# A selective scan's spread transfers on ScalarE's queue in the last image pair

## The chip, the cores and the metric

The program runs on one core of one Trainium2 chip. The metric is the device time of one execution in microseconds (us). Five engines each run their own instruction queue in order: PE (TensorE, matrix multiplies), DVE (VectorE), ACT (ScalarE), POOL (GpSimd) and SP (SyncE, which computes nothing and issues transfers). ACT can issue transfers too. Engines wait for each other, and for transfers, through semaphores.

## The reference

Eight images of 64 channels and 64 x 64 pixels pass through four layers: a bottleneck, two window-attention blocks, a dynamic filter with a convolution, and a vision state-space block. The change lies in the last one, in its selective scan. With `dt` the softplus of a projection of `x`, it computes for 4 directions, 128 channels and 16 states, along 4096 positions:

```
def step(h, inp):
    u_t, dt_t, B_t, C_t = inp
    h = h * jnp.exp(dt_t[..., None] * A) + dt_t[..., None] * B_t[:, :, None, :] * u_t[..., None]
    return (h, jnp.einsum('bkcn,bkn->bkc', h, C_t))
```

Every state of a channel needs that channel's `dt` and `dt*x`. After the scan the four directions are summed, normalized, gated and projected, and a last block (called `back` below) mixes the channels.

## The kernel before

Images are worked in four pairs. For pair p, `scans(p, ...)` (L1657) runs the scan of its two images while a generator named `beside` issues other work between the steps: the `back` of the pair before, and the `front` (all layers ahead of the scan) of the pair after. In the last pair there is no next pair, so `beside` holds only `back(2)`; when it is used up, `self.turn` becomes 0 (L1690) and tiles from `bank` alternate between the two sets of PSUM buffers. `late`, the last pair's own `back(3)`, is advanced only in the last seven units (L1693) and after the loop.

The scan of a pair is 64 units: 2 images x 4 directions x 8 chunks of 512 positions. A unit has 8 steps; a step handles 2 of the 16 states on 128 partitions (64 channels x 2 states, in two halves `j` of 512 columns). What one unit needs is made during the unit before it, after its first three steps (L1695):

- `load` (L1704), after step 0: a transfer of `x` into `xs`.
- `inputs` (L1709), after step 1: PE projects `x`; ACT makes the softplus (L1717, L1720) and copies `dt` into the tile `du1` (L1721); PE and ACT make the rows of B and C, which go to memory (`rows`, L1727).
- `spread` (L1729), after step 2: DVE multiplies `dt*x` into the second half of `du1` (L1733), then two transfers of 512 KB each (L1737) copy every channel of `du1` to two partitions of the tile `du`, one transfer for each half g of the channels. `du` has two buffers, `du1` one.

In each step, `fetch` (L1739) issues the broadcast transfers of the rows of B (three steps ahead) and of C (two steps ahead), with four buffers each; POOL multiplies B by `dt*x` from `du` (`products`, L1752, two steps ahead); ACT makes `exp(dt*A)` from `du` into a PSUM bank `dad` (L1774); DVE runs the recurrence (L1777); ACT copies the end of the recurrence to `carry` (L1785); DVE or POOL multiplies by C (L1791); PE sums over the states (L1803). After step 2 DVE gathers the unit before (L1816 to L1821).

All transfers of the scan are issued from SP's queue: B, C, `xs`, `rows`, `du` and the results. The order within each engine's queue isn't the written one alone: a planner lays the instructions out at build time by its own estimate of when each can start, and the earlier written one first where several can. [...]

Of the kernel before, what the change touches and what calls it, by code (L numbers as in the profile page):

```python
# [15 lines left out]
B, C, HH, WW = 8, 64, 64, 64  # L16
# [1143 lines left out]
class _Direct:  # L1160
# [568 lines left out]
    def spread(self, u):  # L1729

        nc, one = self.nc, u["one"]
        du = u["du"] = self.sw.tile([P, GRP, 2, TD], F32, name="du", tag="du")
        nc.vector.tensor_tensor(one[:, 1], u["pd"], u["x"], ALU.mult)  # L1733
        m = P // GRP
        for g in range(GRP):
            src = one[m * g : m * g + m].rearrange("c q t -> c (q t)").unsqueeze(1).to_broadcast([m, GRP, 2 * TD])
            nc.sync.dma_start(du[:, g].rearrange("p q t -> p (q t)"), src)  # L1737

    def fetch(self, i, st, s):  # L1739

# [213 lines left out]
```

## Time and profile before

| what | us |
|---|---|
| median of 3 executions | 12660.21 (12629.84 to 12661.61) |
| the profiled execution, of its own | 12668.15 |
| its span, first to last instruction | 12666.3 |

The last pair, by stretches of the profiled execution. Times are from the start of the span; shares are busy time over the stretch. Units are counted by their L1733, 64 in the pair.

| stretch, us | units prepared in it | beside the scan | DVE | POOL | ACT |
|---|---|---|---|---|---|
| 10422 to 10920 | 16 | first part of `back(2)` | 88% | 82% | 54% |
| 10920 to 11460 | 16 | its convolutions | 92% | 75% | 53% |
| 11460 to 11620 | 5 | its end | 89% | 82% | 50% |
| 11620 to 12310 | 21 | nothing | 80% | 79% | 44% |
| 12310 to 12530 | 6 | `back(3)` begins | 90% | 81% | 57% |

Over the whole span DVE is busy 67%, POOL 59%, ACT 55%, PE 77%. SP issues 512 `du` transfers, 128 of them in the last pair, with a median of 5.9 us from issue to landing. A line of the timeline names the start, the duration, the engine, the line of the program, what is written from what, and in brackets how long the engine had been idle and what ended that. SPq is SP's queue of transfers.

### The profile page before, as it was taken

What the parts mean: (1) busy time and instruction counts of PE and PEld (TensorE: products, weight loads), DVE (VectorE), ACT (ScalarE), POOL (GpSimd) and SP (SyncE); (2) the same over time, 40 slices, a digit from 0 to 9 for tenths busy, and PEclk for the clock granted to TensorE, in tenths of its full rate; (3) what the DMA queues carried; (4) which work ended last, traced back from release to release, by engine and by line L of the source; (5) the groups of instructions that cost most, each with busy time, mean ns of one, the idle gap of its engine ahead of it and who ended that gap; (6) DMA issues with size and microseconds to landing.
All of it is one profiled execution on the core that took longest, in us unless ns stands there. A gap on an engine that the chain in (4) does not pass through costs nothing. (4 is left out here: it accounts for less than half of the span.)

```text
span 12666.3 us, 142495 instructions
## 1 busy us (share of the span) xinstructions
PE 9810.4 (77%) x46358; PEld 3319.4 (26%) x46358; DVE 8518.4 (67%) x10259; ACT 7014.7 (55%) x15694; POOL 7504.2 (59%) x3844
## 2 busy tenths in 40 slices
PE   9888879987888667997988756998888855555456
PEld 2255222223342112222443211222433211111111
DVE  0122257678776776668776779467777678988878
ACT  5533237665654655666565555666666465455444
POOL 0000017677775683667676676467777568778774
PEclk9966779998888778998888867998888967777767
DMA  0000025554443463445443455344444356556554
GB/s 19 1 1 1 5 91 150 145 149 136 136 129 102 142 192 95 136 139 151 122 129 114 125 180 157 88 138 148 129 131 136 101 169 190 170 169 186 172 170 131
DMA packets 779701, 1575.82 MB, mean 124 GB/s; under 512 B 89280, under 2 KB 89408, under 8 KB 778176
## 3 DMA queue, kind: packets, MB, share of 16 engines
q1 hardware_dynamic: 754752, 1510.30, 40.1%
q10 hardware_dynamic: 24192, 56.32, 1.2%
q8 instruction: 367, 6.01, 0.2%
q14 instruction: 390, 3.19, 0.1%
HBM read 1197.16 MB, written 100.66 MB: 102 GB/s over the span
## 5 line engine op out<-in xcount | busy, mean ns | idle before, releaser
L1752 POOL TENSOR_TENSOR vd<-B,du 128x1024 f32<-128x1024 f32 x2048 | 4797.6, 2362 | 3280.0 <-DMA B<-rows 2024.8
L1803 PE MATMUL yd<-vd,pack 128*64 128x512 f32 x8192 | 2923.6, 736 | 939.0 <-POOL vd L1791 593.2
L1774 ACT ACTIVATE dad<-du,As 128x512 f32<-128x512 f32 x4096 | 2732.3, 682 | 1051.1 <-DVE hd L1777 409.0
L1777 DVE TENSOR_TENSOR_SCAN hd<-dad,carry,vd 128x512 f32<-128x512 f32 x1992 | 2498.3, 1268 | 485.6 <-ACT dad L1774 333.8
L1791 POOL TENSOR_TENSOR vd<-hd,C 128x512 f32<-128x512 f32 x1290 | 1646.5, 1281 | 1032.7 <-DVE hd L1777 1004.2
L1777 DVE TENSOR_TENSOR_SCAN dad<-dad,carry,vd 128x512 f32<-128x512 f32 x1592 | 2005.7, 1274 | 169.5 <-ACT dad L1774 165.4
L1788 POOL TENSOR_TENSOR vd<-hd,C 128x1024 f32<-128x1024 f32 x491 | 1158.3, 2359 | 712.9 <-DVE hd L1777 364.4
L1307 ACT ACTIVATE e<-s 128x512 f32<-128x512 f32 x2048 | 1201.6, 591 | 624.1 <-PE s L1301 622.3
L1301 PE MATMUL s<-X 64*128 64x512 f32 x4096 | 1429.7, 645 | 79.8 <-ACT e L1307 59.8
L1803 PEld LDWEIGHTS yd<-vd,pack 128*64 128x64 f32 x8192 | 658.3, 159 | 2796.3 <-issue 1197.4
L1791 DVE TENSOR_TENSOR vd<-dad,C 128x512 f32<-128x512 f32 x1824 | 1208.8, 674 | 268.0 <-ACT carry L1785 251.3
L1293 PE MATMUL po<-e,VT 128*64 128x512 f32 x4096 | 1209.8, 625 | 16.9 <-ACT e L1307 10.2
L1458 PEld LDWEIGHTS w_av<-vals,wide 64*64 64x64 f32 x16384 | 674.9, 172 | 201.8 <-ACT wide L1448 75.1
L1458 PE MATMUL w_av<-vals,wide 64*64 64x9 f32 x16384 | 703.3, 223 | 20.5 <-ACT wide L1448 20.3
L1785 ACT ACTIVATE carry<-hd 128x1 f32<-128x1 f32 (+1 forms) x1559 | 307.7, 200 | 690.8 <-DVE hd L1777 677.3
L1301 PEld LDWEIGHTS s<-X 64*128 64x128 f32 x4096 | 391.4, 186 | 1107.1 <-issue 834.5
L1785 ACT ACTIVATE carry<-dad 128x1 f32<-128x1 f32 x1594 | 268.3, 169 | 681.0 <-DVE dad L1777 671.0
L1715 PE MATMUL pdd<-xs,xdt 128*128 128x512 f32 x512 | 375.5, 823 | 326.1 <-issue 103.0
L1239 PE MATMUL pv<-n_sq,pack 128*128 128x512 f32 x576 | 361.8, 713 | 154.6 <-ACT n_sq L1237 142.8
L1448 ACT ACTIVATE wide<-wide 128x512 f32<-128x512 f32 x512 | 309.7, 626 | 279.3 <-DVE wide L1447 278.9
L1575 PE MATMUL acc<-taps,pack 128*128 128x512 f32 x576 | 374.1, 782 | 107.6 <-DVE taps L1574 107.2
L1447 DVE TENSOR_TENSOR wide<-w_s,bias 128x512 f32<-128x512 f32 x512 | 328.4, 680 | 191.2 <-PE w_s L1430 187.1
(246 smaller groups left out, 10620.4 us busy)
## 6 DMA issues: line engine op xcount, KB each, us to landing
B<-rows SPq DMA_DIRECT2D x2048, 256.0 KB, 3.5
C<-rows SPq DMA_DIRECT2D x2048, 256.0 KB, 3.5
du<-du SPq DMA_DIRECT2D x512, 512.0 KB, 5.9
xs<-xt SPq DMA_DIRECT2D x128, 256.0 KB, 3.7
xs<-xc SPq DMA_DIRECT2D x128, 256.0 KB, 3.8
xc<-xcv ACTq DMA_DIRECT2D x64, 256.0 KB, 2.0
zs<-z ACTq DMA_DIRECT2D x64, 256.0 KB, 3.8
xt<-XT ACTq DMA_DIRECT2D x32, 512.0 KB, 4.8
```

What stands on the lines that cost most here:

```text
L1293: nc.tensor.matmul(po[half[im]], lhsT=VT[:, t, half[im]], rhs=es[im], start=(t == 0), stop=(t == 31))
L1301: nc.tensor.matmul(ss[im], lhsT=at(half[im], t), rhs=X[half[im], jc * CH : (jc + 1) * CH], start=True, stop=True)
L1307: nc.scalar.activation(e, ss[im], AF.Exp, scale=C**-0.5, accum_out=parts[:, im, t, jc : jc + 1])
L1458: nc.tensor.matmul(self.av[half[im], x % 4 + j, h, :], lhsT=es[h // 4][half[im], j, h % 4, :], rhs=V[half[im], x + j, h, :], start=True, s ...
L1715: nc.tensor.matmul(pd, lhsT=net.xdt[:, k, :], rhs=x, start=True, stop=True)
L1752: self.nc.gpsimd.tensor_tensor(v, self.twice(st["B"]), self.units[i // 8]["du"][:, :, 1], ALU.mult)
L1774: nc.scalar.activation(da, u["du"][:, j, 0], AF.Exp, scale=net.As[:, k, n : n + 1])
L1777: nc.vector.tensor_tensor_scan(along(to), along(da), along(v[:, j]), first, ALU.mult, ALU.add)
L1785: nc.scalar.activation(cs, ends, AF.Copy)
L1788: st["w"] = nc.gpsimd.tensor_tensor(v, h, self.twice(CC), ALU.mult)
L1791: m = engine.tensor_tensor(v[:, j], hs[j], CC, ALU.mult)
L1803: m = nc.tensor.matmul(u["y"][self.HALF[j]], lhsT=w["fold"], rhs=st["v"][:, j], start=(i % 8 == 0), stop=(i % 8 == 7))
```

## The change

The two transfers of `spread` are issued from ACT's queue for images 6 and 7, which make up the last pair; for the others they stay on SP's.

```diff
         nc.vector.tensor_tensor(one[:, 1], u["pd"], u["x"], ALU.mult)
         m = P // GRP
+        queue = nc.scalar if u["image"] >= B - 2 else nc.sync
         for g in range(GRP):
             src = one[m * g : m * g + m].rearrange("c q t -> c (q t)").unsqueeze(1).to_broadcast([m, GRP, 2 * TD])
-            nc.sync.dma_start(du[:, g].rearrange("p q t -> p (q t)"), src)
+            queue.dma_start(du[:, g].rearrange("p q t -> p (q t)"), src)
```

Sizes, sources, destinations and the number of transfers are the same.

## The prediction

> **What bounds the kernel now.** Only the last pair's 64 units change, so I read that stretch alone: first who waits for whom, then the timeline of one unit. The waits between 11300 and 12300 us (engine and line, what it waited for; total us, times, longest):
>
> ```profile
> ACT dad L1774 <- DMA du<-du: 197.8, 45, 10.4
> POOL vd L1752 <- DMA du<-du: 145.0, 22, 7.7
> DVE vd L1791 <- ACT carry L1785: 125.6, 26, 7.0
> ```
>
> The spread transfer is what ACT and POOL wait for longest, and DVE waits for ACT about as long. The same view from 10300 to 11300 us gives POOL 25.3 us on `du` and ACT none worth listing: the wait belongs to the stretch with nothing beside the scan. One unit of it in the timeline:
>
> ```profile
> 11831.21 0.67 DVE L1733 TENSOR_TENSOR du<-pdd,xs 128x512 f32<-128x512 f32 x1
> 11831.81 2.45 DVE L1777 TENSOR_TENSOR_SCAN dad<-dad,carry,vd 128x512 f32<-128x512 f32 x2
> 11831.91 0.69 ACT L1774 ACTIVATE dad<-du,As 128x512 f32<-128x512 f32 x1 [0.96 <-DVE du L1733]
> ...
> 11834.39 0.56 SPq L1744 DMA_DIRECT2D B<-rows  x1
> ...
> 11839.62 0.51 SPq L1744 DMA_DIRECT2D C<-rows  x1
> ...
> 11840.18 0.60 SPq L1744 DMA_DIRECT2D B<-rows  x1
> ...
> 11840.88 1.20 SPq L1737 DMA_DIRECT2D du<-du  x2
> ...
> 11842.14 2.19 SPq L1744 DMA_DIRECT2D C<-rows  x1
> ...
> 11846.43 1.30 ACT L1774 ACTIVATE dad<-du,As 128x512 f32<-128x512 f32 x2 [7.22 <-DMA du<-du]
> ...
> 11847.85 0.69 DVE L1791 TENSOR_TENSOR vd<-dad,C 128x512 f32<-128x512 f32 x1 [5.93 <-ACT carry L1785]
> ...
> 11848.71 2.35 POOL L1752 TENSOR_TENSOR vd<-B,du 128x1024 f32<-128x1024 f32 x1 [6.67 <-DMA du<-du]
> ```
>
> What to see: the source of the spread is complete at 11831.88, but SP issues the transfers at 11840.88, 9.0 us later. SP isn't busy: it stands at a fetch of C whose buffer POOL frees only at 11839.6 (its L1791), and B and `du` are queued behind that. ACT then waits 7.22 us at the next unit's first exponential; the carry copies of the old unit stand behind it in ACT's queue, so DVE, which has old work ready, idles 5.93 us, and POOL 6.67 us.
>
> The timeline also holds the other case:
>
> ```profile
> 11577.07 0.69 DVE L1733 TENSOR_TENSOR du<-pdd,xs 128x512 f32<-128x512 f32 x1
> 11577.81 1.20 SPq L1737 DMA_DIRECT2D du<-du  x2
> 11587.09 2.36 POOL L1752 TENSOR_TENSOR vd<-B,du 128x1024 f32<-128x1024 f32 x1 [0.43 <-DMA B<-rows]
> ```
>
> Here SP was free, the transfers went out 0.05 us after the multiply, landed at about 11585, and neither ACT nor DVE stood still; POOL lost 0.43 us, on B. Going through L1733 and L1737 of the last pair this way: in the 22 units prepared from 11604 to 12325 us the issue comes 7.7 to 11.4 us late, and these units take 32.75 us each (720.5 us from the first L1733 to that of the 23rd). Just before, late and punctual units alternate: the intervals after punctual issues (0.1 to 2.7 us late) are 27.0, 26.7 and 26.3 us, those after late ones (8.1 and 8.8 us) 31.0 and 33.9 us.
>
> **What the Trainium skill says.** "DMA: Bandwidth & Descriptors", section on the anatomy of one DMA: a transfer's wait is done by the issuing sequencer before dispatch, not by the DMA engines. The trace agrees: the 9.0 us above pass ahead of the issue. The same page, "Issuing engines are not separate DMA queues": transfers from SP, ACT and POOL run on the same 16 DMA engines and interleave; another issuer saves only sequencer time. So I count no bandwidth won, only the queueing. Its section on queues and rings says that SP and ACT own one ring each on every DMA engine, served in turn by packets; the trace fits so far as fetches issued behind `du` take 2.2 us to issue (11842.14) where 0.5 is usual, which should go. "Perfetto Trace Analysis", on hardware-generated DMAs, says that the reported interval of an issue is the sequencer's own time; so 2 x 0.6 us is what ACT's queue would be held by each spread.
>
> **The change part by part.**
>
> *Removed from SP:* 128 issues of 0.6 us, on an engine that mostly waits. By itself nothing; B and C move up, and no fetch is issued behind a megabyte.
>
> *Moved to ACT:* two issues a unit, waiting for L1733. Price on ACT: 1.2 us a unit as on SP. (ACT's own 256 KB stores show 0.33 us as median, the 512 KB ones 0.62, so 0.65 to 1.25 us bounds it; I take 1.2.) In the quiet stretch ACT is 44% busy and lies idle 0.96 us until L1733 ends anyway. The next DVE work needing ACT: the two recurrences from 11831.81 have their exponentials already, and the one at 11835.36 needs the exponential of 11831.91, which would run at 33.1 to 33.8. So 0 there, if the planner puts the issues right at L1733.
>
> *Late wait gone:* punctual spreads in this pair (15 of the 64) landed 6.8 to 9.0 us after the multiply, the first half after 4.5 to 7.1. From 11831.9 that means 11836.4 to 39.0 and 11838.7 to 40.9. ACT wants the first half at 11839.2, POOL the whole at 11842.0. Both are met or missed by under 1 us; contention from the fetches can't be seen separately, and the punctual cases had it too.
>
> *What is late next:* without its 5.93 us of idle, that unit's 32.61 us (11815.24 to 11847.85) leave DVE 26.7 us of unbroken work; POOL's stretch from 11816.16 to 11842.04 is 25.9. Those are the floors. The two engines feed each other, and a small B wait appeared in the punctual unit, so I take 27.5 us, between 26.7 and the 28.6 us that the recurrences of that punctual unit spanned (11565.0 to 11593.6, 2.1 us of it idle). 22 units x (32.75 - 27.5) = 115.5 us. The two late units before them: 31.0 + 33.9 - 2 x 27.5 = 9.9 us. Together -125.
>
> *The other 40 units:* no gain that I count. In the 16 from 10422 the issue is 0 to 9 us late and POOL waits 5.5 us at B behind it, but DVE, 88% busy, waits for ACT, which waits 55.5 us in total at L1717 for PE; an earlier B doesn't end that. There I take +0.5 us a unit, within -2 and +2: ACT's exponentials come close on L1733 and 1.2 us more can show. In the 15 of the convolutions DVE is 92% busy; at 11034.6 the row copy and the exponentials stand right behind L1733 and DVE already waits 1.31 us for them, while at 11279.7 they are done. I take +0.8, within 0 and +2. In the last stretch, +0.5 for five units; the few in between I count at nothing. Sum 8 + 12 + 2.5 = +22.
>
> Net -125 + 22 = -103 on the profiled execution's 12668.15 us: 12565. The median shown lies 8 us under that execution, so 12557, say 12558.
>
> **The rivals.**
>
> *A second wait takes half.* POOL at 25.9 of 27.5 us a unit has little room; SP still stands at fetches of C until POOL frees a buffer, B sits behind them, and POOL may wait for B where it waited for `du`. For: the 0.43 us above, and the 65.5 us of B waits in POOL from 10422 to 10900. Against: there they came behind the `du` issues. With units at 30 us the gain is 22 x 2.75 = 60, less 22: 12668 - 38 - 8 = 12622.
>
> *The move doesn't do what it says.* The planner may set the issues late in ACT's queue, behind exponentials or copies that wait for DVE, or a semaphore shared with an earlier transfer holds them. Then `du` is as late as before: about 12650. Against: nothing on ACT between L1733 and its end needs anything but L1733.
>
> *Slower.* ACT's queue is in order, so from when it reaches the issues until L1733 ends it does nothing else. If the planner sets them ahead of the exponentials of step 3, DVE finds no `dad` after L1733 and idles for 1.2 us of issue plus 0.68 of exponential, about 2 us; beside `back`, whose squares, logarithms and Gelus also stand behind, more. It decides once it costs 125/63 = 2.0 us a unit; at 3 us, 189 - 125 = +64: 12724. For: ACT reaches that place early in the first two stretches. Against: in the quiet stretch and at 12398 the exponentials precede L1733.
>
> **How the numbers follow.** Chances: forecast 0.68, own range 12505 to 12605; second wait 0.15; no effect 0.08; slower 0.09. About 0.3%, or 38 us, is what a measurement can tell from no change, so faster means under 12622. The forecast and over half of the second wait are faster, 0.77; the rest of that and no effect are the same, 0.14; slower 0.09. Range: the floors (22 x 6.05 + 10 = 143), no cost elsewhere and a few us won among the first 16 units give 12500; upward it takes in the second wait and no effect up to 12655, leaving out the slower case and some tail below.
>
> **What would show it.** Right: the `du` issues on ACT within 0.2 us of L1733's end; no wait of 5 us or more for `du` on ACT or POOL between 11600 and 12300; unit spacing there 27 to 28 us; DVE over 93% busy there; the first two stretches as long as before within 2%. Wrong: exponentials that DVE waits for right after the issues, B in the place of `du` in POOL's waits, or ACT idle at the issues ahead of L1733.

## The result, and the profile after

| | median, us | all runs | profiled execution | its span |
|---|---|---|---|---|
| before | 12656.5 | 12629.84 to 12661.61 | 12668.15 | 12666.3 |
| after | 12524.3 | 12509.1 to 12532.55 | 12516.79 | 12515.0 |

The ratio is 0.9898, with a 95% interval of 0.988 to 0.9916: 1% faster. The granted TensorE clock is 0.82 in both profiles. The new line in the source moves everything below it by one: L1737 is now L1738, L1752 is L1753, L1774 is L1775, L1777 is L1778, L1785 is L1786 and L1791 is L1792.

First the waits of after between 11300 and 12300 us, the view that the prediction began with (total us, times, longest):

```profile
ACT carry L1786 <- DMA C<-rows: 50.9, 9, 8.0
...
POOL vd L1753 <- DMA du<-du: 30.8, 19, 2.7
...
DVE vd L1792 <- DMA C<-rows: 23.0, 20, 2.5
...
DVE vd L1792 <- ACT carry L1786: 12.0, 13, 2.8
```

ACT's 197.8 us at `du` are gone from the list, POOL's 145.0 have become 30.8 and none is longer than 2.7, and DVE's 125.6 us behind ACT's carry copies have become 12.0. One line is new: ACT standing ahead of carry copies until a fetch of C lands, 50.9 us. A carry copy doesn't read C; the timeline of one unit shows what this is.

```profile
11757.62 1.29 ACT L1775 ACTIVATE dad<-du,As 128x512 f32<-128x512 f32 x2
...
11759.16 0.67 DVE L1733 TENSOR_TENSOR du<-pdd,xs 128x512 f32<-128x512 f32 x1
11759.57 1.74 SPq L1745 DMA_DIRECT2D C<-rows  x2
...
11759.76 2.45 DVE L1778 TENSOR_TENSOR_SCAN dad<-dad,carry,vd 128x512 f32<-128x512 f32 x2
11760.19 3.41 ACTq L1738 DMA_DIRECT2D du<-du  x2
...
11762.12 1.25 DVE L1778 TENSOR_TENSOR_SCAN hd<-dad,carry,vd 128x512 f32<-128x512 f32 x1
11763.30 2.43 DVE L1778 TENSOR_TENSOR_SCAN dad<-dad,carry,vd 128x512 f32<-128x512 f32 x2
11763.64 0.23 ACT L1786 ACTIVATE carry<-dad 128x1 f32<-128x1 f32 x2 [4.73 <-DVE hd L1778]
...
11765.65 1.86 DVE L1792 TENSOR_TENSOR vd<-dad,C 128x512 f32<-128x512 f32 x3
...
11769.11 2.35 POOL L1753 TENSOR_TENSOR vd<-B,du 128x1024 f32<-128x1024 f32 x1 [1.27 <-DMA B<-rows]
```

The multiply ends at 11759.83 and the first transfer goes out 0.36 us later; over the quiet units the mean is 0.10 us, and the prediction had wanted 0.2. ACTq is ACT's queue of transfers. The ACTq line spans 3.41 us for two issues of 0.53: in the trace's events the second goes out at 11763.06, when the semaphore that it is to raise has been released by an earlier transfer, the fetch of C that SP had issued at 11759.57 (landed 11763.04). ACT does nothing for 4.73 us. DVE's recurrences nevertheless follow each other at 11759.76, 11762.12 and 11763.30 without a gap, since all the exponentials that they need were made ahead, the last two at 11757.62.

The quiet stretch as a whole, the 22 units from the 37th to the 59th L1733: length, then busy us (instructions) of PE, PE's weight loads, DVE, ACT and POOL, then clock, DMA share and GB/s. Before:

```profile
11604.00:12325.00 721.00, 367.87 (x796) 82.26 (x792) 580.30 (x618) 320.14 (x766) 567.20 (x308) 0.70 0.56 170
```

After:

```profile
11569.00:12168.00 599.00, 348.49 (x796) 76.15 (x796) 577.61 (x617) 311.92 (x765) 568.19 (x308) 0.69 0.67 205
```

The same work in 122 us less: DVE goes from 80% to 96% busy and POOL from 79% to 95%. From L1733 to L1733 the trace gives this for the pair:

| stretch (units of the last pair) | before, us | after, us | difference |
|---|---|---|---|
| up to the pair's first L1733 | 10422.3 | 10402.9 | -19.4 |
| 16 units beside the first part of `back(2)` | 498.5 | 500.8 | +2.3 |
| 15 beside its convolutions | 538.4 | 520.4 | -18.0 |
| 5 at its end | 144.9 | 144.7 | -0.2 |
| 22 quiet ones | 720.5 | 599.3 | -121.2 |
| 5 beside `back(3)` | 171.6 | 175.1 | +3.5 |
| the rest | 170.1 | 171.8 | +1.7 |

The first row is not put down to the change: up to there SP, ACT, DVE and POOL run the same instructions in the same order in both profiles (13395 on ACT, 8097 on DVE), and the profiles of nine other kernels below that leave that part alone reach this point anywhere from 10360 to 10410 us. The profile of before is the latest of all. The last pair itself gave 132 us.

One more thing differs in the last pair that the diff doesn't show: the planner laid the other engines' work out anew. In after, DVE runs five recurrences right after the multiply in 19 of the 22 quiet units (11759.76 to 11763.30 above). In before it runs two in all 22 and then multiplies by C, as in the punctual unit that the prediction showed:

```profile
11577.66 2.46 DVE L1777 TENSOR_TENSOR_SCAN dad<-dad,carry,vd 128x512 f32<-128x512 f32 x2
...
11580.02 1.28 DVE L1791 TENSOR_TENSOR vd<-dad,C 128x512 f32<-128x512 f32 x2
```

So a part of the gain may be owed to the new order and not to the spread. e4 and e7 below keep two recurrences after the multiply, and help to bound that part.

### The profile page after: what moved, and what is told of

The parts are those of the page before. It is cut to its first block, busy times and chain, and to the rows that moved or that the text cites. A ratio compares the mean times of both kernels' runs of the same rounds, so it can differ in the third digit from the quotient of the medians.

```text
span 12515.0 us, 142739 instructions
## 1 busy us (share of the span) xinstructions
PE 9804.9 (78%) x46358; PEld 3303.1 (26%) x46358; DVE 8519.5 (68%) x10259; ACT 7003.1 (56%) x15694; POOL 7502.7 (60%) x3844
## 5 line engine op out<-in xcount | busy, mean ns | idle before, releaser
L1753 POOL TENSOR_TENSOR vd<-B,du 128x1024 f32<-128x1024 f32 x2048 | 4797.0, 2362 | 3137.6 <-DMA B<-rows 2018.3
L1775 ACT ACTIVATE dad<-du,As 128x512 f32<-128x512 f32 x4096 | 2726.5, 682 | 863.2 <-DVE hd L1778 406.5
L1778 DVE TENSOR_TENSOR_SCAN hd<-dad,carry,vd 128x512 f32<-128x512 f32 x1992 | 2497.8, 1268 | 481.1 <-ACT dad L1775 324.4
L1792 POOL TENSOR_TENSOR vd<-hd,C 128x512 f32<-128x512 f32 x1290 | 1648.8, 1282 | 1032.3 <-DVE hd L1778 1018.2
L1778 DVE TENSOR_TENSOR_SCAN dad<-dad,carry,vd 128x512 f32<-128x512 f32 x1592 | 2003.9, 1274 | 160.8 <-ACT dad L1775 157.5
L1792 DVE TENSOR_TENSOR vd<-dad,C 128x512 f32<-128x512 f32 x1824 | 1207.2, 675 | 147.3 <-ACT carry L1786 112.6
L1293 PE MATMUL po<-e,VT 128*64 128x512 f32 x4096 | 1212.6, 626 | 16.9 <-ACT e L1307 10.2
L1786 ACT ACTIVATE carry<-dad 128x1 f32<-128x1 f32 x1594 | 266.5, 169 | 794.3 <-DVE dad L1778 698.7
L1786 ACT ACTIVATE carry<-hd 128x1 f32<-128x1 f32 (+1 forms) x1559 | 308.1, 200 | 672.7 <-DVE hd L1778 659.2
L1293 PEld LDWEIGHTS po<-e,VT 128*64 128x64 f32 x4096 | 234.8, 136 | 852.8 <-issue 569.8
```

The costliest lines, as they stand in the source:

```text
L1293: nc.tensor.matmul(po[half[im]], lhsT=VT[:, t, half[im]], rhs=es[im], start=(t == 0), stop=(t == 31))
L1753: self.nc.gpsimd.tensor_tensor(v, self.twice(st["B"]), self.units[i // 8]["du"][:, :, 1], ALU.mult)
L1775: nc.scalar.activation(da, u["du"][:, j, 0], AF.Exp, scale=net.As[:, k, n : n + 1])
L1778: nc.vector.tensor_tensor_scan(along(to), along(da), along(v[:, j]), first, ALU.mult, ALU.add)
L1786: nc.scalar.activation(cs, ends, AF.Copy)
L1792: m = engine.tensor_tensor(v[:, j], hs[j], CC, ALU.mult)
```

## The experiments

The main theory: `du` is late because its issue stands in SP's queue behind a fetch of C that waits for a buffer; a queue that is not standing there takes the wait away, and the quiet stretch is then bound by DVE and POOL. All spacings below are of the quiet stretch unless another is named, all differences in the pair are between its first and last L1733 (before 2073.8 us, after 1940.3).

### e1, e2 and e3: other sets of units

The condition of the change, `u["image"] >= B - 2`, becomes `u["image"] == B - 1` in e1 and `u["image"] == B - 2` in e2; in e3 it falls away:

```diff
-            nc.sync.dma_start(du[:, g].rearrange("p q t -> p (q t)"), src)
+            (nc.scalar if u["image"] == B - 1 else nc.sync).dma_start(du[:, g].rearrange("p q t -> p (q t)"), src)
```

> The spread transfers go on ACT's queue for image 7 alone (the last 32 units), image 6 stays on SP. Queue theory (the gain is the punctual spread in the quiet stretch, which lies in image 7): the quiet units fall from 32.75 to about 27.2 us, about -115 us in all, 12530 to 12555. Planner theory (the new order of the whole last pair gives the gain, wherever the transfers are issued): a part of the gain that follows the number of moved units, about -65 us.

> The spread transfers go on ACT's queue for image 6 alone, image 7 stays on SP. Queue theory: the quiet units stay at 32.7 us with the 6 us of idle DVE at each boundary; the time is within -25 and +15 us of before. Planner theory: about half of the gain, -65 us.

> The spread transfers go on ACT's queue in all four pairs. Queue theory: outside the last pair the trace of before has 22 us of waits for du in all, so there is nothing to win there, and ACT, busier with front work, pays 0 to 1.2 us for each of 192 units: between the time of the changed kernel and 200 us above it, 12520 to 12720. If a late spread were a cost in all pairs alike, it would fall well below 12500.

| kernel | median, us | ratio | 95% interval | last pair, us | quiet unit, us |
|---|---|---|---|---|---|
| e1, image 7 alone | 12533.58 | 0.9917 | 0.9901 to 0.9934 | 1953.6 | 27.21 |
| e2, image 6 alone | 12646.0 | 1.0004 | 0.9995 to 1.0013 | 2074.2 | 32.57 |
| e3, all four pairs | 12632.57 | 0.9987 | 0.998 to 0.9995 | 1942.8 | 27.24 |

Image 7 holds the quiet stretch, and moving its issues alone gives 120 of the 134 us, not a half, so the queue theory's forecast holds and the planner theory's, by the number of moved units, doesn't. (e1 has after's order on DVE in the quiet units, so it can't part the spread from that order.) Moving image 6's alone shortens the convolution stretch by 19 us, 538.4 to 519.2, and gives it all back in the next five units, 144.9 to 164.0: those are issued from SP again, and come 7.4 us late where they came 4.0 late before.

e3 answers whether the other queue is good in itself. The last pair is as short as after, but the first three are longer, by L1733: 2701.7, 2904.8 and 2912.4 us against after's 2680.1, 2872.4 and 2860.3. That is 106 us over 192 units; the whole time lies in the range that was expected. Their issues were only 1.0 us late on SP, so there was little to win; POOL's waits for `du` outside the last pair come to 54 us in before, where the expectation had counted 22. What it cost is in the waits over these three pairs (1832 to 10349 us in after, 1830 to 10461 in e3). After:

```profile
DVE hd L1778 <- ACT dad L1775: 335.0, 195, 10.7
DVE dad L1778 <- ACT dad L1775: 173.1, 157, 7.8
...
POOL vd L1753 <- DMA du<-du: 49.9, 19, 10.4
```

e3:

```profile
DVE hd L1777 <- ACT dad L1774: 401.0, 226, 9.1
DVE dad L1777 <- ACT dad L1774: 257.8, 160, 8.8
...
POOL vd L1752 <- DMA du<-du: 385.5, 44, 12.3
```

DVE waits 151 us more for ACT's exponentials; ACT, which also does the attention and layer work of the next pair there, now stands at issues too. `du` isn't even earlier: the whole of it lands 8.6 us after the multiply (median) where it was 7.2, because the second issue is 2.6 us late on average against 1.8, and POOL waits 336 us more for it. DVE doesn't pass that on: its recurrences in `hd` waited 143.4 us for POOL's products in after and 65.0 in e3. So the trace puts the loss at ACT. The planner's order changed in these pairs too, though, and no run parts the two. The net cost, 0.55 us a unit, is of the size of the 0.5 to 0.8 us that the prediction set as ACT's price.

### e4: SP again, but the spread ahead of the fetches

All transfers stay on SP, and in the last pair each later fetch is ordered behind the spread.

```diff
+            m_ = nc.sync.dma_start(du[:, g].rearrange("p q t -> p (q t)"), src)
+            self.spread_last = m_ if u["image"] >= B - 2 else None
...
-        self.nc.sync.dma_start(t, row.unsqueeze(0).to_broadcast([64, 2, TD]))
+        d = self.nc.sync.dma_start(t, row.unsqueeze(0).to_broadcast([64, 2, TD]))
+        if self.spread_last is not None:
+            self.net.behind(d, self.spread_last)
```

> All spread transfers stay on SP's queue, but in the last pair the later fetches of B and C are ordered behind them in that queue. Queue theory (only the place behind the standing fetches made them late): du is issued within 0.2 us of L1733's end, quiet units 27 to 28.5 us, 12520 to 12570, as good as the changed kernel within 0.4%. Rival (a queue of its own is needed, since now the fetches stand behind a wait for DVE and POOL runs out of B): POOL waits for B by several us a unit, quiet units over 30 us, 12600 or more.

Measured: 12555.45 us, ratio 0.9932 (0.9915 to 0.9948), 28.54 us a quiet unit: what the queue theory expected, at the upper end of its spacing. A unit of its timeline:

```profile
11660.12 0.69 DVE L1733 TENSOR_TENSOR du<-pdd,xs 128x512 f32<-128x512 f32 x1
...
11660.72 2.46 DVE L1780 TENSOR_TENSOR_SCAN dad<-dad,carry,vd 128x512 f32<-128x512 f32 x2
...
11660.87 1.20 SPq L1737 DMA_DIRECT2D du<-du  x2
11662.12 2.13 SPq L1745 DMA_DIRECT2D B<-rows  x1
...
11663.08 1.28 DVE L1794 TENSOR_TENSOR vd<-dad,C 128x512 f32<-128x512 f32 x2
...
11664.35 2.10 SPq L1745 DMA_DIRECT2D C<-rows  x1
```

The spread is 0.06 us late in the quiet units, ACT issues none of it, and both halves have landed 7.0 us after the multiply (9.0 in after). DVE runs two recurrences after the multiply in all 22 quiet units, as in before. So about two thirds of the gain, 0.0068 of 0.0102, came from the place in the queue, without another queue and without DVE's new order. Where the remaining 1.3 us a quiet unit lie isn't shown. The trace points at what is now behind the spread: B and C take 2.1 us to issue there instead of 0.5, and POOL waits for B (from 11500 to 12200 us):

```profile
POOL vd L1755 <- DMA B<-rows: 34.8, 16, 4.2
```

DVE in turn waits 37.6 us for POOL's products in e4's quiet stretch, and not at all in after's. In the quiet stretch 41 fetches take over 1.5 us to issue in e4, 43 in before and 14 in after. The other candidate is DVE's new order, which after has and e4 hasn't.

Ahead of the quiet stretch the two queues seem to differ: the 16 first units take 480.3 us in e4 and 500.8 in after, the 15 beside the convolutions 545.3 against 520.4. The two stretches are better read together. Over the 31 units before takes 1036.9 us, e4 1025.6, e6 (below) 1021.7 and after 1021.2. All three gain; how the gain divides between the two stretches differs from kernel to kernel.

### e6: one half on each queue

```diff
+            (nc.scalar if u["image"] >= B - 2 and g == 0 else nc.sync).dma_start(du[:, g].rearrange("p q t -> p (q t)"), src)
```

> In the last pair the first of the two transfers goes on ACT's queue, the second stays on SP's. Queue theory: POOL's products need both halves, so POOL waits as in before for the second, and ACT's exponentials for the second half of the channels too: quiet units 31 to 33 us, at most 35 us won. Rival (half the megabyte off SP's queue is enough, since the fetches behind it issue faster): about half of the gain, -60 us.

Measured: 12612.22 us, ratio 0.9978 (0.997 to 0.9986), 31.47 us a quiet unit, as the queue theory expected. The first half goes out 0.1 us after the multiply, the second, on SP, 7.8 us; POOL needs both halves at once, and its wait between 11500 and 12200 us stays what it was (118.8 us in before):

```profile
POOL vd L1752 <- DMA du<-du: 120.7, 21, 6.1
```

For POOL the spread is as early as its later half.

### e7: the slower rival, made

The changed kernel with the exponentials of step 3 ordered behind the issues, the order that the prediction's slower rival feared.

```diff
...
-            nc.scalar.activation(da, u["du"][:, j, 0], AF.Exp, scale=net.As[:, k, n : n + 1])
+            ex = nc.scalar.activation(da, u["du"][:, j, 0], AF.Exp, scale=net.As[:, k, n : n + 1])
+            if i % 8 == 3 and self.spread_last is not None:
+                net.behind(ex, self.spread_last)
```

> The changed kernel, with the exponentials of step 3 ordered behind the two issues in ACT's queue: the slower rival of the prediction, made on purpose. If an in-order hold of ACT at the issues costs what was worked out there, DVE idles after L1733 for at least 1.2 us of issue and 0.7 us of exponential in nearly all 64 units: 2 us a unit, +128 us over the changed kernel, about 12650; if ACT also stands between the two issues (2 to 3 us there in the trace of the changed kernel), 4 to 5 us a unit, 12750 to 12830. If ACT's place doesn't matter: within 30 us of the changed kernel.

Measured: 12541.05 us, ratio 0.9923 (0.9907 to 0.994), 28.49 us a quiet unit. One unit:

```profile
11722.29 0.69 DVE L1733 TENSOR_TENSOR du<-pdd,xs 128x512 f32<-128x512 f32 x1
...
11723.14 1.19 ACTq L1737 DMA_DIRECT2D du<-du  x2
...
11724.38 1.91 ACT L1775 ACTIVATE dad<-du,As 128x512 f32<-128x512 f32 x3 [3.27 <-POOL vd L1753]
11725.17 2.35 DVE L1780 TENSOR_TENSOR_SCAN dad<-dad,vd 128x512 f32<-128x512 f32 x2 [2.19 <-ACT dad L1775]
```

DVE idles 2.19 us after the multiply, 2.25 on the mean of the quiet units where it is 0.00 in after: the rival's 1.2 + 0.68 was well sized. But the unit grows by only 1.25 us, because the 0.97 us that DVE idles elsewhere in after are gone. The first 36 units together grow by 6.7 us and the pair by 29.0, to 1969.3 us, where the expectation had 128 or more if the hold costs. In this order the change still pays.

e7 also answers the question of DVE's order: its 616 DVE instructions of the quiet stretch stand in exactly the order of before, and with ACT's loss included it still wins 4.3 of the 5.5 us a unit.

### e8 and e12: carry copies first, on the kernel before

Is it rather ACT's order, with the old unit's carry copies behind the new unit's exponentials, that makes the late `du` expensive? Both kernels leave the spread on SP. e8:

```diff
...
+            ex = nc.scalar.activation(da, u["du"][:, j, 0], AF.Exp, scale=net.As[:, k, n : n + 1])
+            if i % 8 == 0 and self.carried is not None:
+                net.behind(ex, self.carried)
...
+                self.carried = nc.scalar.activation(cs, ends, AF.Copy)
+                if u["image"] < B - 2 or i % 8 < 7:
+                    self.carried = None
```

> The kernel before, with the first two exponentials of a unit ordered behind the last carry copy of the unit before, in the last pair; no transfer is moved. It takes away what made DVE stand still while old work was ready. If DVE's 6 us at the boundary are the cost: quiet units near 28 us, about -100 us. If the late spread itself is (POOL's products wait for it just as long, and POOL's 25.9 us of work plus 6.7 us of wait is the unit too): quiet units stay over 31 us, at most 35 us won.

Measured: 12635.73 us, ratio 1.0002 (0.9993 to 1.0011), 32.34 us a quiet unit. It first looked as if ACT's order didn't matter. But the edit hadn't made the order it was to make: the new unit's own first carry copy clears `carried`, so that the exponential of its second half wasn't held. The waits of DVE in e8's quiet stretch (11550 to 12260 us) show it:

```profile
DVE vd L1795 <- ACT carry L1787: 84.2, 19, 6.2
```

In before (11604 to 12325 us) these waits, and POOL's, were:

```profile
DVE vd L1791 <- ACT carry L1785: 121.0, 20, 7.0
...
POOL vd L1752 <- DMA du<-du: 140.7, 20, 7.7
```

Most of DVE's wait was still there, so e8 doesn't decide. e12 repairs it:

```diff
...
+            ex = nc.scalar.activation(da, u["du"][:, j, 0], AF.Exp, scale=net.As[:, k, n : n + 1])
+            if i % 8 < 3 and self.carried is not None:
+                net.behind(ex, self.carried)
...
+                copied = nc.scalar.activation(cs, ends, AF.Copy)
+                if u["image"] >= B - 2 and i % 8 == 7:
+                    self.carried = copied
```

> In e8 only the first of the new unit's exponentials was ordered behind the old unit's last carry copy, and the second still ran ahead of it, so DVE went on waiting for carry copies (84 us in the quiet stretch). Here all exponentials of the new unit's first three steps are ordered behind that copy, on the kernel before. If the lateness of du on its own is the bound, through POOL's products, DVE's wait for carry copies goes under 20 us but the quiet units stay at 31.5 us or more and the total within 25 us of before. If the order on ACT is what makes the lateness expensive, DVE's idle time of some 5.5 us a unit shrinks by half or more, units come to 30 us or less, and the total falls by 60 us or more.

Measured: 12606.4 us, ratio 0.9973 (0.996 to 0.9985), 30.74 us a quiet unit. DVE's and POOL's waits from 11560 to 12260 us:

```profile
DVE vd L1795 <- ACT carry L1787: 6.8, 12, 1.4
```

```profile
POOL vd L1752 <- DMA du<-du: 84.0, 18, 7.4
```

It falls between the two theories. With the issue still 7.3 us late (9.7 before) and on SP, e12 wins 2.0 of the 5.5 us a unit that the change wins: DVE's wait for carry copies is all but gone, and POOL's wait for `du` falls from 140.7 to 84.0 us. So over a third of what the late `du` cost could be had back with the issue still 7.3 us late; the larger part stayed. That ACT's order alone did this isn't shown, for the planner laid DVE's and POOL's work out anew in e12 as well: in 8 of the 22 units fewer than two recurrences follow the multiply.

### e9 and e10: the changed kernel again, and a mix

e9 is the changed kernel. e10 takes e4's order for the first 16 units of the pair and ACT's queue for the other 48.

```diff
...
+            on_sp = u["image"] == B - 2 and u["nth"] < 2
+            q_ = nc.scalar if u["image"] >= B - 2 and not on_sp else nc.sync
+            m_ = q_.dma_start(du[:, g].rearrange("p q t -> p (q t)"), src)
+            self.spread_last = m_ if on_sp else None
...
```

> The changed kernel once more, as the neighbour of e10 on the same chip. Expected 12515 to 12535 us, ratio to before 0.988 to 0.992; last pair about 1940 us from its first to its last multiply of dt*x, its first 16 units 500 us, its quiet 22 units 600 us.

> In the first 16 units of the last pair the spread stays on SP, with B and C of later steps ordered behind it; the other 48 units of the pair issue it from ACT. If the stretches add up, the first 16 units take the 480 us that e4 showed (500 in the changed kernel) and the rest stays as in the changed kernel, quiet units at 27.2 us: about 20 us below the changed kernel, 12505 us or so. If instead time won there only slides into the convolutions, as in e2, the 15 units after them get longer by about as much and the total equals the changed kernel's within 8 us.

e9: 12503.03 us (12496.51 to 12505.62), ratio 0.989 (0.9874 to 0.9907), 12 us under the range expected for it. e10: 12499.49 us (12490.53 to 12506.84), ratio 0.9887 (0.987 to 0.9903). The 16 units do take 479.6 us instead of 500.4, but the convolutions after them take 526.2 instead of 521.8, and three other stretches together 4.8 us more; the pair ends at 1930.4 us against 1942.0. The 3.5 us between the medians lie inside the spread of either kernel. Whether the mix beats the changed kernel is not settled.

SP's stand itself was taken away by no run. e5, the kernel before with a fifth buffer for C, was expected at about 29.5 us a quiet unit and has no result: the fifth buffer doesn't fit into SBUF beside the other tiles (17.25 KB per partition are wanted where 15.25 are left).

## Why the prediction was right

*Queueing, not bandwidth.* "So I count no bandwidth won, only the queueing", the prediction drew from the Trainium skill ("DMA: Bandwidth & Descriptors", the section that issuing engines are not separate DMA queues). e3 agrees: where the issue stood only 1.0 us in SP's queue, the other queue saved nothing. e4 bounds it: two thirds of the gain came on the same queue. The last third may be queueing too, now of B and C behind the spread, or DVE's new order; no run took either alone. The prediction had fetches of 2.2 us to issue behind `du` that should go, and 43 of over 1.5 us become 14. The page's remark that another issuer saves only sequencer time names the thing saved, but here that time is standing behind another issue in a queue, 9.7 us a unit, and not the 0.6 us of an issue.

*The late wait and the next floor, 27.5 us.* No wait of 5 us for `du` is left in the quiet stretch, and the first issue is 0.1 us late on the mean; 27.24 us a unit were measured (27.21 in both e9 and e1). e12 adds what the prediction described and didn't price: the part of the loss that can be had back by working on at the old unit. The prediction took the order on DVE as given and didn't foresee that the planner would change it; e4 and e7 leave about 1.3 us of the 5.5 a unit for this, if the parts simply add up. DVE's busy time is 26.4 us a unit before and 26.3 after; the prediction had read 26.7 as its unbroken work and added the feeding between DVE and POOL. 121.2 us came where 115.5 were counted.

*The two late units before them, 9.9 us.* Units of 31.1 and 33.8 us became 27.5 and 26.8: 10.6 us. In the table they don't show, since the unit that starts their stretch took 34.9 us instead of 27.0.

*ACT's price in the quiet stretch.* It costs nothing there, as said (DVE waits 0.8 us for exponentials in after's whole quiet stretch), but the size was wrong: the two issues hold ACT for 4.1 us there on the mean and not for 1.2. Cover was ACT's idle time and the exponentials made ahead; in e7 that cover is gone and DVE pays 2.2 us.

*The other 40 units, +22.* This term failed: "no gain that I count" was wrong. The first 16 cost 2.3 us where 8 were taken, the last five 3.5 where 2.5 were, and the 15 beside the convolutions gave 18.0 where they were to cost 12; they became 3.3% shorter, where the prediction had wanted both stretches within 2%. The spread was late there too, by 5.2 and 1.7 us on the mean in before, and with that gone the gain outweighed what ACT's issues cost: over the 31 units together DVE's idle time fell from 103 to 90 us (92 in e4), and POOL's wait for `du` in the convolutions from 18.0 us to nothing. Each kernel that makes the spread or half of it punctual gains 11 to 17 us over these 31 units, e4 on SP included, and e10 with both queues 31. Why after's gain shows in the convolutions and e4's in the first 16 is open; the planner's order differs between them there, and no run took it alone.

*The sum.* -103 was predicted for the pair and -132 measured, 29 us apart. The convolutions make 30 of these; the quiet stretch and the first 16 units, each 6 us better than taken, are offset by the five units after the convolutions, which stayed as they were where 10 was to be won, and by small change at the end. So the number came close because the largest term was right to 6 us, and not because errors cancelled: the wrong term lies on the side of a larger gain. Another 19 us between the two profiled executions lie ahead of the pair, and the same kernel varies about as much: its median was 12524.3 us here and 12503.03 in e9.

*The rivals.* The second wait didn't take half: the waits of POOL's products for B from 11300 to 12300 us come to 16.8 us, 10.2 of them in one. In e4, where B stands behind the spread, this rival shows on a small scale (34.8 us). "a semaphore shared with an earlier transfer holds them" was half right, for the second issue alone, 3.7 us late on average in the quiet stretch. POOL still waits 23.4 us for `du` there, but DVE not at all for POOL. The slower order is priced by e7.

## What to carry to other kernels

Read how long an issue stands in its queue after its source is complete: the wait that this lateness causes on the busiest engine, times the units where nothing covers it, is what another queue or another place in the same queue can bring; here 9.7 us of lateness cost 5.5 us a unit, and where the issue was 1.0 us late the move only cost. Try the order within the queue too: here it gave two thirds of the gain without another engine's queue. Before moving issues, look whether the new engine has its next outputs ready, as ACT had its exponentials. Compare the order of the other engines' instructions before and after, since a planner may change it along with the queue. And read neighbouring stretches together, for time won in one can turn up in the next (e2, e10).

## What the runs showed of the hardware and had not been expected

The transfers of SP's and ACT's queues share eight completion semaphores in this program, and an issue waits until the transfer that used its semaphore last has landed: of 5572 issues with such a predecessor in the profile of after, none goes out before. In all 22 quiet units ACT's second issue goes out 0.02 us after the landing of a fetch of C that SP had issued and that it has no data in common with, on the mean 3.0 us after the first issue's end; in 26 of the first 31 units the planner puts other ACT work between the two. This is read from the trace's events. In e7's quiet units, where the issues come ahead of ACT's exponentials, the second follows 0.1 us after the first and the whole lands after 7.8 us instead of 9.1. What the stand costs in after can't be read from that, since e7's order costs something of its own.

Fetches can also take longer to issue while a spread is in flight. All 43 fetches of over 1.5 us in before's quiet stretch, and all 14 in after's, were issued between the issue and the landing of a spread transfer; with none in flight the mean is 0.53 us in both. In after the 14 go out on SP 1.1 to 1.8 us after a spread issue on ACT and take up to 2.4 us (7 such fetches in e9), so a separate queue lessens this but doesn't end it.
